# An attention and feed-forward block on one core: load order, maxima turned in blocks on VectorE, and value products in pairs

## The chip, the cores and the metric

The kernel runs on one core of a Trainium2 chip. The metric is the device time of one execution in microseconds; of several runs the median is taken. TensorE (PE) multiplies, VectorE (DVE) and ScalarE (ACT) read its results in PSUM, GpSimd (POOL) works on SBUF alone here, and SyncE (SP) issues most of the DMAs.

## The reference

x has four batches of 512 rows with 512 features. All of it is fp32.

```python
q = rotary((x @ Wq + bq) in 16 heads of 32);  k = rotary(x @ Wk + bk);  v = x @ Wv + bv   # one k and v for all heads
attn = softmax(q k^T / sqrt(32));  ctx = attn @ v
x = layernorm(x + ctx @ Wo + bo)
quantize(w) = clip(round(w / (mean(|w|) + 1e-8)), -1, 1)
h = sigmoid(x @ quantize(w1).T) * (x @ quantize(w2).T)      # 1408 hidden features
x = layernorm(x + h @ quantize(w3).T)
```

## The kernel before

The kernel is written out step by step; every instruction is pinned to the order in which the program issues it, so each engine and each DMA queue works strictly in that order. A helper records the instructions, so most of them have line 75 (VectorE, ScalarE, GpSimd), 80 (matmuls), 83 (DMAs of SyncE) or 86 (transposes) in the profile.

**Steps.** A step (b, c, t) is one of 64: batch b, a group c of four heads, a block t of 128 keys. The main loop (lines 855 to 894) does in each step: the scores of all 512 queries against the 128 keys for four heads (`scores`, line 404), then the value products of the step before (`weigh`, line 445), and in batch 0 the sums of its exponentials by matmuls against ones (`count`, line 454). For later batches GpSimd adds the exponentials up (`total`).

**Scores.** `scores` fills two PSUM tiles `ps` of two heads each: 32-row matmuls against kT, and onto them a two-row matmul with `negm`, which takes the row maximum off. ScalarE then writes the exponentials `es` (1024 columns at a time). `weigh` multiplies `es` with v into four column strips of `acc`; `count` does the same into `den`.

**Maxima.** The maximum of each query's scores is found seven steps ahead (LEAD = 7, `find_maxima`, line 812): matmuls into `pmax`, and a reduction `mx` on VectorE. For batch 0 these are 32-row matmuls (`row_maxima`), later full ones from a split q (`maximum`, line 371). Four chunks of 128 queries per step are taken as two pairs; a pair has a tile of the same two-buffer pool as `ps` (tag "sc"). A single chunk takes the tile of tag "den" (one buffer). Once the next-to-last projection is past (`batches[-1].done < NC` is false, from about step 26) the maxima stand 1-2-1 with fill work between them (lines 886 to 893).

**Spreading the maxima.** `spread` (line 385) turns the 128x16 maxima of a group by a PE transpose into a tile `pm` of the two-buffer pool "mm"; ScalarE negates them, VectorE takes the rest that the rounded type leaves, and two DMAs carry them through DRAM into `negm`, two rows for each head.

**Fill.** Between these, `fill.draw(pace)` takes pieces of other work, each about 1.8 us of PE: projections of later batches (`project_in`: pk, pq, followed by a rotation of four or five VectorE operations, `turn`, line 238), the output projection `po`, and the feed-forward products `gu` and `po`. All their PSUM tiles come from "mm". `quantize(n)` (line 777) draws jobs that load, sum and quantize the feed-forward weights: ACT makes `sgn`, VectorE makes `raw` from it; after step 16 `sgn` is put into the PSUM bank "den" (line 210). `due()` starts late work such as `normalize` (line 461; reductions `part`, small operations `few`), `store_q` and loads, by counted slots, twice a step.

**Start.** 24 fp32 matmuls of ones warm PE up (`WARM`, lines 53 and 152). Meanwhile SyncE issues all loads in the order of lines 129 to 144: biases, k/v weights, four chunks of xT, the first q weights, cos, sin, the rest.

The main loop's part for the maxima and the fill, as before:

```python
        if batches[-1].done < NC:

            find_maxima(n + LEAD, 0, 1)
            begin_middle()
            due()
            find_maxima(n + LEAD, 2, 3)
            quantize(1)
            fill.draw(pace)
            quantize(1 if b == 0 or n % 3 == 0 else 0)
```

Of the kernel before, what the change touches and what calls it, by code (L numbers as in the profile page):

```python
# [10 lines left out]
F32 = mybir.dt.float32  # L11
F32R = mybir.dt.float32r
BF16 = mybir.dt.bfloat16
I32 = mybir.dt.int32
AF = mybir.ActivationFunctionType
ALU = mybir.AluOpType
# [4 lines left out]
P = 128  # L21
HD = 32
# [6 lines left out]
def postln_block(  # L29
# [15 lines left out]
    nc = tc.nc  # L45
    B, T, D = x.shape
    NC = D // P
    NT = T // P
    NF = wf.shape[1]
    NG = P // HD  # L50
    SCALE = 1.0 / float(HD) ** 0.5
    W = 512
    WARM = 24

    const = ctx.enter_context(tc.tile_pool(name="const", bufs=1))
    small = ctx.enter_context(tc.tile_pool(name="small", bufs=2))
# [10 lines left out]
    pin = tc.keep_in_program_order  # L67
# [14 lines left out]
    def move(out, in_):  # L82
        pin(nc.sync.dma_start(out=out, in_=in_))  # L83

    def transpose(out, in_, identity):
        pin(nc.tensor.transpose(out, in_, identity))
# [31 lines left out]

    chunks = iter([(b, c) for b in range(B) for c in range(NC)])

    def load_xT(n):

        for _ in range(n):
            b, c = next(chunks, (None, None))
            if b is not None:
                batches[b].xT.append(work.tile([P, T], F32, tag="xT", name="xT", bufs=6))
                move(batches[b].xT[c], xT[b, :, c, :])

    move(bkv_sb, bkv)
    move(bq_sb, bq)  # L130
    move(wkv_sb, wkv)
    load_xT(NC)
    move(wq_sb[0], wq[:, 0])
    move(cos_sb, cos)
    move(sin_sb, sin)
# [22 lines left out]
    def quantized():  # L158

        order = ((0, False), (1, False), (0, True), (2, False), (1, True), (2, True))
        jobs = [(m, last, f) for m, last in order for f in range(NF)]

        means = {}
        for n, (m, last) in enumerate(order):
            if not last:
                for k, step in ((2, 0), (6, 1), (10, 2)):
                    means[(n + 1) * NF + k] = (m, step)
        raws, part, row, pg, hi, waiting = {}, {}, {}, {}, {}, []  # L170

        def load(k):
            if k < len(jobs):
                m, _, f = jobs[k]

                tag, bufs = ("wd", 5) if k % 2 else ("wg", 4)
                raws[k] = wp.tile([P, W], F32, tag=tag, name="raw", bufs=bufs)
                pool.dma_start(out=raws[k], in_=wf[m, f])

        def mean(m, step):  # L180
            if step == 0:
                row[m] = small.tile([P, 1], F32, tag="row", name="row")
                dve.tensor_reduce(row[m], part[m], AX.X, ALU.add)
            elif step == 1:
                pg[m] = ps_mm.tile([P, 1], F32, tag="mm", name="pg")
                mm(pg[m], ones, row[m], True, True)
                gamma = small.tile([P, 1], F32, tag="gamma", name="gamma")
                act.activation(gamma, pg[m], AF.Identity, scale=1.0 / (NF * W * P), bias=eps_q)
                row[m] = gamma
            else:  # L190
                hi[m] = small.tile([P, 1], F32, tag="hi", name="hi")
                act.mul(hi[m], row[m], 0.5)

        AHEAD = 4
        for k in range(AHEAD):
            load(k)
        for k, (m, last, f) in enumerate(jobs):
            load(k + AHEAD)
            if k in means:
                mean(*means[k])  # L200
            raw = raws.pop(k)
            if not last:
                if f == 0:
                    part[m] = small.tile([P, NF], F32, tag="part", name="part", bufs=3)
                junk = work.tile([P, W], BF16, tag="th", name="junk")
                act.activation(junk, raw, AF.Abs, accum_out=part[m][:, f : f + 1])
            else:
                if now > PER:

                    sgn = ps_acc.tile([P, W], F32, tag="den", name="sgn")  # L210
                else:
                    sgn = work.tile([P, W], BF16, tag="th", name="sgn")
                act.activation(sgn, raw, AF.Sign, bias=hi[m])
                dve.scalar_tensor_tensor(raw, raw, hi[m], sgn, ALU.is_gt, ALU.min)
                waiting.append((kept[m][f], raw))
            if len(waiting) > 2 or k + 1 == len(jobs):
                for w, q in waiting[: 1 if k + 1 < len(jobs) else 3]:
                    pool.dma_start(out=w.bitcast(F32), in_=q)
                del waiting[:1]
            yield  # L220
# [164 lines left out]
    def spread(b, c):  # L385


        s = batches[b]
        pm = ps_mm.tile([NG * NT, P], F32, tag="mm", name="pm")
        transpose(pm, s.mx[c].rearrange("p i t -> p (i t)"), ident)  # L390
        m = small.tile([NG * NT, 2, P], F32R, tag="m", name="m")
        mH, mL = m[:, 0, :], m[:, 1, :]
        act.mul(mH, pm, -1.0)
        dve.scalar_tensor_tensor(mL, pm, -1.0, mH.bitcast(F32), ALU.mult, ALU.subtract)
        s.negm[c] = work.tile([P, T], F32R, tag="negm", name="negm", bufs=3)
        yield
        rows = dram.tile([2, NG, T], F32, tag="rows", name="rows", bufs=3)
        move(rows.rearrange("n i (t k) -> (i t) n k", k=P), m.bitcast(F32))
        yield
        for n in range(2):  # L400
            move(s.negm[c].bitcast(F32).rearrange("(i r) k -> i r k", r=HD)[:, n], rows[n])
        yield

    def scores(b, c, t):
# [40 lines left out]
    def weigh(b, c, t, es):  # L445
        s = batches[b]
        if t == 0:
            s.acc = ps_acc.tile([P, T], F32, tag="acc", name="acc")
            s.ctxT[c] = work.tile([P, T], F32, tag="ctxT", name="ctxT", bufs=6)
        columns(s.acc, s.v[:, t, :], es, t == 0, t == NT - 1)  # L450
        if t == NT - 1:
            act.copy(s.ctxT[c], s.acc)

    def count(b, c, t, es):

        s = batches[b]
        if t == 0:
            s.den = ps_acc.tile([P, T], F32, tag="den", name="den")
        columns(s.den, ones[:, 0:HD], es, t == 0, t == NT - 1)
# [317 lines left out]
    def quantize(n):  # L777
        for _ in range(n):
            next(weights, None)
# [12 lines left out]
    def due():  # L792

        nonlocal slot
        slot += 1
        for entry in list(late):
            if slot >= entry[0] and next(entry[1], "end") == "end":
                late.remove(entry)
# [13 lines left out]
    def find_maxima(k, *chunks):  # L812

        if k >= len(steps):
            return
        b, c, i = steps[k]
        if chunks[0] == 0:
            ask(k + HEADS)
            while batches[b].done <= c or (b and k not in heads):
                if batches[b].done <= c:  # L820
                    fill.one()
                else:
                    begin_middle()
                    due()
                    ask(k)
        if b == 0:
            row_maxima(b, c, i, chunks[0] // 2)
        else:
            maximum(b, c, i, chunks, heads[k])
        if i == NG - 1 and chunks[-1] == NT - 1:  # L830

            late.insert(0, (slot + (1 if now < 0 else 2), spread(b, c)))
# [18 lines left out]
            move(bo_sb, bo.partition_broadcast(P))  # L851
        quantize(3)

    last = None
    for n, (b, c, t) in enumerate(steps):
        now = n
        pace = (1.8, 3.8, 4.8, 4.6)[b]
        if t == 1 and PER <= n + NT - 1 < len(steps):
            load_q(*steps[n + NT - 1][:2])
        es = scores(b, c, t)  # L860
        if last is not None:
            weigh(*last)
        if last is not None and last[0] == 0:
            count(*last)
        last = (b, c, t, es)
        if n == NC * NT // 2:

            late.append((slot, load_x(0)))
        if t == NT - 1:
            begin = slot + 3  # L870
            late.append((begin, normalize(b, c)))
            if c == NC - 1:
                late.append((begin + 7, feed(b)))
                if b > 0:
                    late.append((slot + 6, load_x(b)))
        if batches[-1].done < NC:

            find_maxima(n + LEAD, 0, 1)
            begin_middle()
            due()  # L880
            find_maxima(n + LEAD, 2, 3)
            quantize(1)
            fill.draw(pace)
            quantize(1 if b == 0 or n % 3 == 0 else 0)
        else:
            find_maxima(n + LEAD, 0)
            fill.draw(0.4 * pace)
            find_maxima(n + LEAD, 1, 2)
            begin_middle()
            due()  # L890
            fill.draw(0.3 * pace, True)
            find_maxima(n + LEAD, 3)
            fill.draw(0.3 * pace)
        due()
    weigh(*last)
    now = len(steps)
    while fill.gens or fill.urgent or late:
        fill.draw(3.0)
# [66 lines left out]
```

## Time and profile before

| what | before |
|---|---|
| three runs | 670.8, 672.12, 674.28 us |
| profiled execution, its own time | 672.56 us |
| its span, first to last instruction | 670.8 us |
| granted TensorE clock, mean | 0.997 |
| DMA moved, mean rate | 107.78 MB, 161 GB/s |
| PE matmuls of gate, up (`gu`) | 704 records, 172.9 us busy |
| `pmax` full, 32-row | 192 and 128 records, 75.2 and 25.7 us |
| `acc`, `den` | 512 and 128 records, 68.2 and 16.7 us |
| `pm` transposes | 16 records, 4.4 us |
| DVE reductions `mx` | 159, 158.1 us |

An fp32 matmul has two records, an fp32r one has one. A busy time is the union of the spans of a group, so overlapping matmuls are not counted twice. A line of the timeline has start, duration, engine, line, operation, the tile written and the tiles read, shapes, and how many; in brackets the idle time of the engine before it and what ended that. Times are in us from the start of the span. A step is named by its number n from 0 to 63, its start is that of its first `ps` matmul.

### The profile page before, as it was taken

Reading aid. Unit: us, or ns where it says so; the run is one execution under the profiler, and the core shown is the slowest. Engines: PE = TensorE matmul, PEld = TensorE weight load, DVE = VectorE, ACT = ScalarE, POOL = GpSimd, SP = SyncE. Lnnn points to the kernel's source line nnn. Section 1 sums busy time; section 2 is a strip of 40 time slices with the busy share of each in tenths; the row PEclk is TensorE's granted clock in tenths of the full one; section 3 lists DMA queues with packets and bytes.
Section 4 is the critical chain, followed back from the end, with each engine's and each line's share of the span. In section 5 each row is a group of like instructions: output and inputs, shape, how many; then the busy total and the mean of one; then the engine's idle time right before and its main releaser. Section 6 shows DMA issues by size and latency. Waiting matters only on the chain.

```text
span 670.8 us, 9406 instructions
## 1 busy us (share of the span) xinstructions
PE 644.7 (96%) x3222; PEld 358.5 (53%) x3222; DVE 430.0 (64%) x619; ACT 282.8 (42%) x441; POOL 324.4 (48%) x414
## 2 busy tenths in 40 slices
PE   9989999999999989999999899999999999999995
PEld 6333333443333355665456466654555685778884
DVE  1896766587787867766666966676635553464335
ACT  1466555655443644333334445233435421234213
POOL 0615334535987776376666375576574802202000
PEclk9999999999999999999999999999999999999998
DMA  8755668688575286355132456351232364236531
GB/s 283 248 192 175 205 199 261 186 286 276 162 245 172 92 259 202 116 169 162 54 84 82 125 164 215 124 172 29 73 100 67 126 217 148 79 109 213 183 107 63
DMA packets 60671, 107.78 MB, mean 161 GB/s; under 512 B 14592, under 2 KB 15360, under 8 KB 60624
## 3 DMA queue, kind: packets, MB, share of 16 engines
q1 hardware_dynamic: 52560, 81.10, 38.5%
q0 software_dynamic: 7920, 25.96, 11.8%
q8 instruction: 25, 0.41, 0.3%
q14 instruction: 22, 0.18, 0.1%
q10 hardware_dynamic: 144, 0.13, 0.1%
HBM read 84.06 MB, written 23.10 MB: 160 GB/s over the span
## 4 chain that ended last, share of the span: by engine, by line
PE 81%; DVE 9%; DMA 4%; ACT 3%; issue 2%; SPq 1%; POOL 0%; DVEq 0%; ACTq 0%; POOLq 0%
PE gu L80 23%; PE po L80 19%; PE ps L80 11%; PE pmax L80 8%; PE acc L80 7%; PE pq L80 7%; DVE mx L75 3%; PE den L80 2%; DMA wg<-w 2%; ACT es L75 2%; PE pk L80 1%; DVE xt L75 1%; PE warm L80 1%; SPq L83 1%; DMA xT<-in_xT 1%
## 5 line engine op out<-in xcount | busy, mean ns | idle before, releaser
L75 DVE TENSOR_REDUCE mx<-pmax 128x1 f32<-128x512 f32 (+1 forms) x159 | 158.1, 1007 | 81.3 <-PE pmax L80 81.1
L75 ACT ACTIVATE es<-ps 128x1024 f32<-128x1024 f32 x128 | 124.2, 1022 | 141.9 <-PE ps L80 133.9
L80 PE MATMUL gu<-y,wg 128*128 128x512 f32 x704 | 172.9, 395 | 2.0 <-DMA wg<-w 1.1
L80 PEld LDWEIGHTS gu<-y,wg 128*128 128x128 f32 x704 | 131.1, 188 | 38.4 <-issue 4.7
L75 POOL TENSOR_TENSOR total<-total,es 128x512 f32<-128x512 f32 x96 | 123.8, 1319 | 45.2 <-ACT es L75 45.1
L80 PE MATMUL po<-wd,h 128*128 128x512 f32 x352 | 87.0, 395 | 4.2 <-DVE y L75 2.9
L75 POOL TENSOR_TENSOR total<-es 128x512 f32<-128x512 f32 x48 | 60.5, 1290 | 55.8 <-ACT es L75 55.8
L80 PE MATMUL pmax<-kr,qr 128*128 128x512 f32 x192 | 75.2, 455 | 3.7 <-ACT es L75 2.2
L80 PEld LDWEIGHTS po<-wd,h 128*128 128x128 f32 x352 | 64.9, 188 | 22.5 <-DVE y L75 4.6
L75 ACT CAST h<-hw 128x512 fp32r<-128x512 f32 x44 | 27.3, 620 | 100.7 <-DVE hw L75 100.7
L80 PE MATMUL acc<-es,v 128*32 128x512 f32 x512 | 68.2, 605 | 0.0
L80 PEld LDWEIGHTS pmax<-kr,qr 128*128 128x128 f32 x192 | 33.6, 188 | 57.0 <-ACT es L75 20.9
L75 DVE SCALAR_TENSOR_TENSOR hw<-th,gu 128x512 f32<-128x512 f32 x44 | 30.2, 687 | 46.9 <-PE gu L80 46.8
L80 PE MATMUL po<-wo_sb,ctxT 128*128 128x512 f32 x128 | 58.9, 593 | 0.3 <-DVE hw L75 0.3
L80 PE MATMUL ps<-negm,ones_r 2*128 2x512 f32 x256 | 58.2, 788 | 0.0
L75 DVE SCALAR_TENSOR_TENSOR xt<-po,xt 128x512 f32<-128x512 f32 x48 | 32.8, 684 | 38.1 <-PE po L80 38.1
L75 DVE TENSOR_TENSOR h<-hw,h 128x512 fp32r<-128x512 f32 x44 | 42.1, 957 | 21.7 <-ACT h L75 21.4
L80 PE MATMUL ps<-qT,kT 32*128 32x512 f32 x384 | 55.6, 640 | 0.0
L75 POOL DMA_DIRECT2D raw<-in_wf x66 | 36.1, 549 | 37.4 <-DMA w<-raw 26.7
L80 PE MATMUL pq<-xT,wq_sb 128*128 128x512 f32 x112 | 53.0, 601 | 1.0 <-ACT v L75 1.0
L75 ACT ACTIVATE th<-gu 128x512 f32<-128x512 f32 x44 | 26.3, 598 | 49.1 <-PE gu L80 49.0
L80 PEld LDWEIGHTS po<-wo_sb,ctxT 128*128 128x128 f32 x128 | 24.1, 189 | 22.0 <-issue 19.2
(98 smaller groups left out, 639.2 us busy)
## 6 DMA issues: line engine op xcount, KB each, us to landing
wg<-w SPq DMA_DIRECT2D x88, 256.0 KB
raw<-in_wf POOLq DMA_DIRECT2D x66, 256.0 KB, 4.6
qr<-qp SPq DMA_DIRECT2D x96, 128.0 KB
wd<-w SPq DMA_DIRECT2D x44, 256.0 KB
w<-raw POOLq DMA_DIRECT2D x33, 256.0 KB, 4.9
qp<-q SPq DMA_DIRECT2D x48, 128.0 KB
rden<-flat SPq DMA_DIRECT2D x64, 64.0 KB
xt<-in_x SPq DMA_DIRECT2D x16, 256.0 KB
```

The costliest lines, as they stand in the source:

```text
L75: return lambda *args, **kw: pin(getattr(self.engine, name)(*args, **kw))
L80: pin(nc.tensor.matmul(out, lhsT=lhsT, rhs=rhs, start=start, stop=stop))
L83: pin(nc.sync.dma_start(out=out, in_=in_))
```

## The change

- **Warming** is 10 matmuls instead of 24.
- **Loads**: the four xT chunks of batch 0 go alternately on ACT's and SP's queue; the biases follow them on ACT's queue instead of standing first on SP's.
- **Maxima**: VectorE negates the 128x16 maxima, takes the rest, and turns both in 32x32 blocks (`turned`). PE's transpose, the "mm" tile and ACT's operation go. The DMAs carry pieces of 32 numbers.
- **Order of a step**: in batch 0 the fill stands ahead of the maxima in odd steps and behind them in even ones; from batch 1 on (step 16) every step has the 1-2-1 form, with `quantize` in it.
- **Value products**: every even step issues, behind its scores, the products (and sums) of the two steps before; odd steps issue none.
- **`sgn`** after step 16 is a bf16 tile in SBUF (tag "rot_a") instead of the bank "den".

```diff
-    WARM = 24
+    WARM = 10
...
+    def load_xT(n, engines=(nc.sync,)):
...
+                pin(engines[k % len(engines)].dma_start(out=batches[b].xT[c], in_=xT[b, :, c, :]))
...
-    move(bkv_sb, bkv)
-    move(bq_sb, bq)
     move(wkv_sb, wkv)
-    load_xT(NC)
+    load_xT(NC, (nc.scalar, nc.sync))
+    pin(nc.scalar.dma_start(out=bkv_sb, in_=bkv))
+    pin(nc.scalar.dma_start(out=bq_sb, in_=bq))
...
-                    sgn = ps_acc.tile([P, W], F32, tag="den", name="sgn")
+                    sgn = work.tile([P, W], BF16, tag="rot_a", name="sgn", bufs=1)
...
-        pm = ps_mm.tile([NG * NT, P], F32, tag="mm", name="pm")
-        transpose(pm, s.mx[c].rearrange("p i t -> p (i t)"), ident)
-        m = small.tile([NG * NT, 2, P], F32R, tag="m", name="m")
-        mH, mL = m[:, 0, :], m[:, 1, :]
-        act.mul(mH, pm, -1.0)
-        dve.scalar_tensor_tensor(mL, pm, -1.0, mH.bitcast(F32), ALU.mult, ALU.subtract)
+        mx = s.mx[c].rearrange("p i t -> p (i t)")
+        m = small.tile([P, 2, NG * NT], F32R, tag="m", name="m")
+        turned = small.tile([P, HD], F32, tag="turned", name="turned")
+        dve.tensor_scalar(m[:, 0, :], mx, -1.0, None, ALU.mult)
+        dve.scalar_tensor_tensor(m[:, 1, :], mx, -1.0, m[:, 0, :].bitcast(F32), ALU.mult, ALU.subtract)
+        dve.transpose(turned, m.rearrange("p n k -> p (n k)").bitcast(F32))
...
-        rows = dram.tile([2, NG, T], F32, tag="rows", name="rows", bufs=3)
-        move(rows.rearrange("n i (t k) -> (i t) n k", k=P), m.bitcast(F32))
+        rows = dram.tile([P // HD, 2, NG, NT, HD], F32, tag="rows", name="rows", bufs=3)
+        move(rows.rearrange("o n i t k -> (o n i t) k"), turned)
         yield
+        to = s.negm[c].bitcast(F32).rearrange("(i r) (t o k) -> i r t o k", r=HD, t=NT, o=P // HD)
         for n in range(2):
-            move(s.negm[c].bitcast(F32).rearrange("(i r) k -> i r k", r=HD)[:, n], rows[n])
+            move(to[:, n], rows[:, n].rearrange("o i t k -> i t o k"))
...
+    def weigh_held():
+        for one in held:
+            weigh(*one)
+        for one in held:
+            if one[0] == 0:
+                count(*one)
+        held.clear()
...
         es = scores(b, c, t)
-        if last is not None:
-            weigh(*last)
-        if last is not None and last[0] == 0:
-            count(*last)
-        last = (b, c, t, es)
+        if t % 2 == 0:
+            weigh_held()
+        held.append((b, c, t, es))
...
-        if batches[-1].done < NC:
-
+        if b == 0:
+
+            if t % 2:
+                fill.draw(pace)
             find_maxima(n + LEAD, 0, 1)
             begin_middle()
             due()
             find_maxima(n + LEAD, 2, 3)
             quantize(1)
-            fill.draw(pace)
-            quantize(1 if b == 0 or n % 3 == 0 else 0)
+            if t % 2 == 0:
+                fill.draw(pace)
+            quantize(1)
         else:
             find_maxima(n + LEAD, 0)
+            quantize(1)
             fill.draw(0.4 * pace)
             find_maxima(n + LEAD, 1, 2)
             begin_middle()
             due()
+            quantize(1 if n % 3 == 0 else 0)
             fill.draw(0.3 * pace, True)
             find_maxima(n + LEAD, 3)
             fill.draw(0.3 * pace)
         due()
-    weigh(*last)
+    weigh_held()
```

More of the change, by code (lines that the diff above doesn't have):

```diff
@@ L119, in postln_block @@
     chunks = iter([(b, c) for b in range(B) for c in range(NC)])
-    def load_xT(n):
-        for _ in range(n):
+    def load_xT(n, engines=(nc.sync,)):
+        for k in range(n):
             b, c = next(chunks, (None, None))
@@ L126, in load_xT @@
                 batches[b].xT.append(work.tile([P, T], F32, tag="xT", name="xT", bufs=6))
-                move(batches[b].xT[c], xT[b, :, c, :])
-    move(bkv_sb, bkv)
-    move(bq_sb, bq)
+                pin(engines[k % len(engines)].dma_start(out=batches[b].xT[c], in_=xT[b, :, c, :]))
     move(wkv_sb, wkv)
-    load_xT(NC)
+    load_xT(NC, (nc.scalar, nc.sync))
+    pin(nc.scalar.dma_start(out=bkv_sb, in_=bkv))
+    pin(nc.scalar.dma_start(out=bq_sb, in_=bq))
     move(wq_sb[0], wq[:, 0])
@@ L852, in postln_block @@
         quantize(3)
-    last = None
+    held = []
+    def weigh_held():
[5 more added lines that the diff above has]
+        held.clear()
     for n, (b, c, t) in enumerate(steps):
```

## The prediction

> **What bounds the kernel now.** I read the page first, then busy time by stage, then TensorE (PE) and VectorE (DVE) instruction by instruction in two steps of each stage.
>
> ```profile
> PE 644.7 (96%) x3222; PEld 358.5 (53%) x3222; DVE 430.0 (64%) x619; ACT 282.8 (42%) x441; POOL 324.4 (48%) x414
> ```
>
> PE is busy for 96% of the span. "Busy" counts from start to modelled end, so a PE that waits inside a row of matmuls still looks busy, and shares alone do not show what an edit is worth. The next view has the stages that I use: the start (until the first scores), A (steps 0 to 15, batch 0), B (16 to 27), C (28 to 57, the rest of the maxima), and the end.
>
> ```profile
> core 0: us, PE busy (x) PEld busy (x) DVE busy (x) ACT busy (x) POOL busy (x), PEclk, DMA share, GB/s
> 0.00:48.20 48.20, 44.48 (x163) 21.42 (x163) 30.67 (x42) 19.61 (x52) 14.64 (x33) 1.00 0.74 252
> 48.20:154.80 106.60, 105.64 (x613) 40.14 (x612) 75.03 (x105) 62.52 (x106) 47.23 (x67) 1.00 0.67 213
> 154.80:244.50 89.70, 84.25 (x404) 33.95 (x403) 71.86 (x102) 43.42 (x62) 71.30 (x87) 1.00 0.63 200
> 244.50:489.20 244.70, 238.75 (x1253) 137.65 (x1253) 164.41 (x225) 97.77 (x131) 145.61 (x154) 1.00 0.42 128
> ```
>
> In A and B, DVE is 70% and 80% busy. There it can be what PE waits for. One step of A, on PE, and the maxima that DVE takes beside it:
>
> ```profile
> 130.66 1.06 PE L80 MATMUL acc<-es,v 128*32 128x512 f32 x8
> 131.54 1.04 PE L80 MATMUL den<-es,ones 128*32 128x512 f32 x8
> 132.51 1.20 PE L80 MATMUL pmax<-kr,qr 128*128 128x512 f32 x4
> 133.55 1.88 PE L80 MATMUL pq<-xT,wq_sb 128*128 128x512 f32 x4
> 135.35 1.13 PE L80 MATMUL ps<-room,kT 32*128 32x512 f32 x6
> ...
> 136.99 1.06 PE L80 MATMUL acc<-es,v 128*32 128x512 f32 x8
> ```
>
> ```profile
> 133.28 2.35 DVE L75 TENSOR_REDUCE mx<-pmax 128x2 f32<-128x1024 f32 x2 [3.31 <-PE pmax L80]
> ```
>
> The reader is to see a ring. `pmax` and `ps` share two PSUM buffers. From `pmax` (132.51) DVE needs until 135.63 for both maxima; only then may the second `ps` tile be written, and `acc` starts 1.34 later, at 136.99. So from `pmax` to the next step's `acc` it takes 4.48 us, whatever PE does in between: `pq` (1.81) and the scores (1.30) fit in. For the maxima of batch 0 (32-row matmuls) the same distance is 4.88 (78.81 to 83.69). The step is this distance plus `acc` and `den`, 1.85.
>
> **Stage A.** The order of instructions of the changed kernel shows its pairs. Even step: scores, 8 `acc`, 8 `den` matmuls, `pmax`, half a projection. Odd step: scores, half a projection, `pmax`, and then at once the next even step's scores. From the rows: two `acc` and two `den` together are 3.57 (4 x 0.86 streamed, 0.13 less than 2 x 1.85); `pmax` to the end of the odd scores 4.48; half a projection 1.81; `pmax` to the even `acc` again 4.48. Sum 14.34, against 2 x (1.85+4.48) = 12.66. The projection of the odd step used to lie beneath the ring and now lies ahead of it: +1.68 a pair. Over the seven pairs of steps 2 to 15: three with 4.88 twice, one mixed, three with 4.48 twice, 45.4+14.8+43.0 = 103.2. To this I add 1.2 for the negation and turning of the maxima, which in steps 5, 9 and 13 stands between the two reductions (0.4 each, see below), and 1.2 for four pairs in which a weight's `raw` (0.74) is queued ahead of them (0.3 each). 105.6; the trace has 93.0 from 63.5 to 156.5. Step 1 gains 0.3. **A: +12.3.** In this 93.0 the losses by the transpose `pm` (it splits four concurrent matmuls into two groups: step 5 took 7.96, its neighbours 6.6 and 6.4) are already inside.
>
> **Stage B.** Now the maxima stand 1-2-1 between fill work, with the single ones in the `den` bank. That takes the waits for exponentials away: step 21 took 7.57, a step of C with the same content in 1-2-1 form (38) took 6.85. Without new waits B would take 12 scores of 1.30, 6 `acc` pairs of 1.88, one `den` pair of 1.74, maxima of 1.12 a step and the trace's 43.4 of fill (0.9 of it the wait of step 16's single `pmax` until ACT has copied `den`): 85.4 for 89.3, so -3.9. But the order on DVE puts a whole rotation between the maxima of the first chunk and those of the pair:
>
> ```profile
> 136.22 0.74 DVE L75 SCALAR_TENSOR_TENSOR a<-pq,bq_sb,cos_sb 128x512 f32<-128x512 f32 x1
> ...
> 137.62 0.76 DVE L75 SCALAR_TENSOR_TENSOR pq<-pq,bq_sb,sin_sb 128x512 f32<-128x512 f32 x1
> 138.47 0.69 DVE L75 TENSOR_TENSOR q<-a,pq 128x512 f32<-128x512 f32 x1
> ```
>
> From 136.22 to 139.16 a rotation is 2.94; it starts when PE is at the pair's `pmax`, and the pair's reduction (1.22) comes behind it, 4.3 us after that `pmax`. PE is back at the second `ps` after 2.57. That is 1.7 lost in step 16, 2.5 in 17 (the rotation of k has five instructions, 3.6), 1.2 in 18 and 3.5 in 19, where the second half of the pair's cover has no fill. Steps 20, 22 and 24 have `part` (1.24), statistics (0.87) or the rotation ahead of the last single maximum: 1.3, 0.4 and 2.1 at the following `pmax`; 2 more in 25 and 26; 0.9 is a longer wait for `xT` in 17. These are 15.6; where one wait takes up another, 13.1 are left, so the whole of it gives +9.2. Bounds -3.9 and +9.2; the stalls are read from the order, so I take near the upper end, **B: +8**.
>
> **Stage C.** Three parts. First, `pm` goes:
>
> ```profile
> 256.58 0.27 PE L86 MATMUL pm<-ident,mx 128*16 128x128 f32 x1
> 257.13 1.65 PE L80 MATMUL gu<-y,wg 128*128 128x512 f32 x6 [0.28 <-DVE hw L75]
> ```
>
> It takes one of two `mm` banks, so the next `gu` waits for DVE. The steps with it are longer than those without by 0.71, 0.62, 0.11, 0.62, 0.63, 0.63, 0.66 and 0.9: -4.9. Second, pairing: one `acc` group alone is 1.00, and 0.88 when another follows. 37 groups remain before, 38 in 19 pairs after: 37.0 against 35.7, -1.3. Third, what the removed `acc` covered in odd steps. The single `pmax` behind it needs the `den` bank, so the last reduction of the step before:
>
> ```profile
> 252.76 0.68 DVE L75 TENSOR_REDUCE mx<-pmax 128x1 f32<-128x512 f32 x1
> ```
>
> ```profile
> 417.29 0.50 PE L80 MATMUL pmax<-kr,qr 128*128 128x512 f32 x1 [0.64 <-DVE mx L75]
> ```
>
> In step 49 this wait exists already, behind `acc`. Without `acc`, PE arrives 1.30 after its scores began. In steps 29, 31, 39, 41, 43 and 45 the reduction ends 1.83, 1.75, 2.16, 1.76, 1.72 and 1.48 after it (29: scores 251.6, reduction until 253.44): waits of 0.63, 0.55, 0.96, 0.56, 0.52, 0.28, and 1.05 more than now in 49 and 53. +5.6; it is 0 if DVE's order is kinder, 11.2 if every wait doubles. **C: -0.6.**
>
> **Start.**
>
> ```profile
> 1.50 8.43 PE L80 MATMUL warm<-ones 128*128 128x128 f32 x48 [1.50 <-POOL ones L75]
> 9.77 3.60 PE L80 MATMUL pk<-xT,wkv_sb 128*128 128x512 f32 x8
> ```
>
> `pk` stands behind the warming matmuls, and the chain to the first maxima behind `pk`. Of 48 warming records 20 stay; at the first ones' spacing (14 in 3.0 us) PE is free at 5.9. The last `xT` chunk landed at 9.01 in the trace; with two queues and without two small loads ahead it lands about 0.9 earlier, so `pk` could end at 9.0 instead of 13.2. Nothing gained and 4.4 gained (with 0.7 for a `pm` at 37.0) are the bounds. The first matmuls ran at half pace: 14 records in the first 3.0 us, 22 in the last 2.2, and the pace changed 5.9 us after the first one, when the changed kernel's warming is just over. So `pk` starts at that half pace; I take **-3.5**.
>
> [...]
>
> **The small parts.** `sgn` in SBUF instead of PSUM: DVE's `raw` takes 0.74 in steps 12 to 16 with an SBUF `sgn` and 0.74 in steps 18 to 24 with the PSUM one: nothing. The turned maxima: ACT loses 0.27, DVE has three operations instead of one of 0.27; the nearest rows are `few` on 128x16 (0.24) and this `m`, so I take 0.2 each, 0.3 to 0.4 more in one step of four, counted in A. Their DMA now moves 128-byte pieces (128, then 2 x 64) instead of 512 and 2048; it is issued at 258.42 and 262.72 for scores at 273.6, so 10 us hide it. If that cover went, its chunk's scores would wait. Nothing is queued behind it on SP that is due sooner than before. Four loads move from SP's queue to ACT's ahead of its first work, at about 0.45 each by SP's rows; ACT's first use of them is at 13.4, which hides that. End: same work, 0.
>
> **Sum**, on the profiled execution's 672.56 (span 670.8): -3.5 +12.3 +8 -0.6 = 688.8; the median is 0.4 lower, so **688.4**.
>
> **Rivals.** (1) Faster: the ring's 4.48 is no floor, since PE's own work between (1.03+1.81+1.30) is 4.14, and DVE is soon enough when the projection is moved. Then A is -3.5 (0.9 by pairs, 2.6 by `pm`), B -3.9, C -6.2, start -3.5: 655. It decides if `pmax` to `acc` in odd steps is under 2.8. Against it: 2.35 of DVE and 1.34 behind it are measured. 0.1. (2) Only A loses, and neither B nor C waits: 672.6-3.5+12.3-3.9-6.2 = 671. 0.1. (3) A and C as forecast, B without waits: 677. 0.2. (4) All at the bad ends, start -0.5, B +9.2, C +5: 698.7. 0.1. Forecast, 683 to 694: 0.5. The range 674 to 697 holds the forecast, (3) and half of (4). This kernel can be told from no change by about 0.5% (3.4 us): faster 0.1, same 0.1, slower 0.8.
>
> **What would show it.** Right: in A odd steps that end with `pmax` directly ahead of `ps`, and 2 us of missing PE work there, pairs of 14 to 15.5; in B DVE's rotation between two `mx`; in C `pmax` waiting for `mx` in odd steps; no `gu` waiting behind `pm`. Wrong: pairs of A under 13, or a start that is not 2 us shorter.

## The result, and the profile after

The changed kernel takes 715.76 us (median of 6 runs, 709.35 to 717.52) against 671.66 us (6 runs on the same chip): ratio 1.0633, 95% interval 1.0598 to 1.0667. The profiled execution took 717.52 us, its span is 715.7, and TensorE's mean granted clock is 0.961 instead of 0.997. The direction was forecast, the size was not: 688.4 was said, and the range ended at 697.

From the page of the changed kernel:

```profile
PE 665.4 (93%) x3178; PEld 368.3 (51%) x3178; DVE 450.3 (63%) x661; ACT 280.5 (39%) x425; POOL 329.0 (46%) x414
```

PE is 20.7 us longer busy for the same products. No new work explains that. The view by stage (us; busy time of PE, PEld, DVE, ACT, POOL with counts; then the granted clock) says where to look:

```profile
0.00:44.80 44.80, 42.20 (x134) 18.07 (x134) 30.70 (x44) 19.43 (x51) 14.64 (x33) 1.00 0.79 271
44.80:177.30 132.50, 119.47 (x593) 43.06 (x592) 76.60 (x113) 62.32 (x102) 46.77 (x65) 0.90 0.56 176
177.30:287.20 109.90, 93.96 (x408) 38.79 (x408) 84.89 (x118) 43.66 (x60) 75.22 (x89) 0.94 0.51 158
287.20:532.10 244.90, 236.17 (x1245) 141.50 (x1244) 170.12 (x241) 95.82 (x123) 145.00 (x153) 0.99 0.42 128
532.10:715.70 183.60, 173.64 (x801) 126.92 (x800) 87.95 (x148) 59.31 (x92) 47.36 (x77) 0.98 0.40 129
```

The length of each stage, against the forecast:

| stage | before | after | difference | forecast |
|---|---|---|---|---|
| start | 48.2 | 44.8 | -3.4 | -3.5 |
| A (steps 0 to 15) | 106.6 | 132.5 | +25.9 | +12.3 |
| B (16 to 27) | 89.7 | 109.9 | +20.2 | +8 |
| C (28 to 57) | 244.7 | 244.9 | +0.2 | -0.6 |
| end | 181.6 | 183.6 | +2.0 | 0 |
| span | 670.8 | 715.7 | +44.9 | +16.2 |

A and B have the whole miss, and they have the lowest clock. PE's waits, summed (us, times, longest):

```profile
PE ps L80 <- DVE mx L75: 18.4, 15, 3.4
PE pmax L80 <- DVE mx L75: 11.8, 13, 1.7
```

Before, `ps` had no such row, and `pmax` waited 1.1 us in all for `mx`. So the new waits are those that were forecast, on VectorE's maxima. But they do not account for 44.9 by themselves. One pair of A (steps 5 and 6), on PE:

```profile
91.40 1.13 PE L80 MATMUL ps<-room,kT 32*128 32x512 f32 x4 [1.31 <-DVE mx L75]
93.04 1.22 PE L80 MATMUL ps<-room,kT 32*128 32x512 f32 x2 [0.52 <-DVE mx L75]
...
95.48 3.64 PE L80 MATMUL acc<-es,v 128*32 128x512 f32 x16
98.89 2.33 PE L80 MATMUL den<-es,ones 128*32 128x512 f32 x16
```

and the pair before it (steps 3 and 4):

```profile
78.58 1.92 PE L80 MATMUL acc<-es,v 128*32 128x512 f32 x16
80.32 1.90 PE L80 MATMUL den<-es,ones 128*32 128x512 f32 x16
```

The same 16 matmuls take 3.64 us instead of 1.92. Cut into windows of 3.41 us, the stretch shows why. The columns are: stretch, its length, busy time of PE, PEld, DVE, ACT and POOL with counts, and then the granted clock, the DMA share and GB/s.

```profile
89.40:92.81 3.41, 1.81 (x12) 0.30 (x4) 3.08 (x6) 1.78 (x4) 2.88 (x5) 1.00 0.17 19
92.81:96.23 3.42, 3.19 (x12) 1.04 (x16) 1.50 (x3) 1.02 (x1) 1.03 (x2) 0.52 0.92 305
96.23:99.64 3.41, 3.41 (x20) 0.79 (x16) 0.00 (x0) 0.00 (x0) 0.54 (x1) 0.50 0.90 320
```

In the first window PE waits, and is busy for 1.81 of 3.41 us. In the next two its clock is half. The six runs agree: the quickest, 709.35 us, had a mean clock of 0.974, the slowest, 717.52, 0.961. Such stretches of one or two windows stand in A at 58.8, 92.9, 113.4, 130.5 and 161.2, all on one grid of 3.41 us, 27.3 us together; in B there are 13.7 us. Before, there were none in A, B and C.

### The profile page after: what moved, and what is told of

It reads as the page before. It is cut to its first block, busy times and chain, and to the rows that moved or that the text cites. A ratio compares the mean times of both kernels' runs of the same rounds, so it can differ in the third digit from the quotient of the medians.

```text
span 715.7 us, 9339 instructions
## 1 busy us (share of the span) xinstructions
PE 665.4 (93%) x3178; PEld 368.3 (51%) x3178; DVE 450.3 (63%) x661; ACT 280.5 (39%) x425; POOL 329.0 (46%) x414
## 4 chain that ended last, share of the span: by engine, by line
PE 70%; DVE 19%; DMA 3%; issue 2%; SPq 2%; ACT 2%; POOL 1%; DVEq 0%; ACTq 0%; POOLq 0%
PE gu L80 21%; PE po L80 16%; PE ps L80 9%; PE acc L80 8%; DVE mx L75 7%; PE pmax L80 7%; PE pq L80 4%; SPq L83 2%; PE den L80 2%; PE pk L80 2%; DVE part L75 2%; DVE raw L75 1%; DVE pq L75 1%; DVE xt L75 1%; DVE a L75 1%
## 5 line engine op out<-in xcount | busy, mean ns | idle before, releaser
L80 PEld LDWEIGHTS gu<-y,wg 128*128 128x128 f32 x704 | 132.5, 189 | 35.1 <-issue 2.4
L80 PE MATMUL pmax<-kr,qr 128*128 128x512 f32 x192 | 85.0, 498 | 13.0 <-DVE mx L75 11.6
L80 PE MATMUL po<-wd,h 128*128 128x512 f32 x352 | 89.2, 403 | 3.8 <-DVE y L75 3.4
L80 PEld LDWEIGHTS po<-wd,h 128*128 128x128 f32 x352 | 66.8, 193 | 21.9 <-DVE y L75 6.1
L80 PE MATMUL acc<-es,v 128*32 128x512 f32 x512 | 71.8, 685 | 0.0
L80 PE MATMUL ps<-qT,kT 32*128 32x512 f32 x384 | 63.3, 642 | 7.6 <-DVE mx L75 7.4
L75 ACT CAST h<-hw 128x512 fp32r<-128x512 f32 x44 | 27.3, 620 | 106.4 <-DVE hw L75 106.4
L80 PEld LDWEIGHTS pmax<-kr,qr 128*128 128x128 f32 x192 | 36.3, 192 | 63.1 <-issue 28.7
L80 PE MATMUL ps<-negm,ones_r 2*128 2x512 f32 x256 | 65.1, 783 | 0.0
L80 PE MATMUL po<-wo_sb,ctxT 128*128 128x512 f32 x128 | 60.8, 603 | 0.0
L75 DVE TENSOR_TENSOR h<-hw,h 128x512 fp32r<-128x512 f32 x44 | 37.7, 857 | 21.0 <-ACT h L75 20.7
L75 POOL TENSOR_TENSOR q<-q,q 128x512 fp32r<-128x512 f32 x12 | 15.2, 1264 | 61.3 <-ACT q L75 60.9
```

The source lines that it names most:

```text
L75: return lambda *args, **kw: pin(getattr(self.engine, name)(*args, **kw))
L80: pin(nc.tensor.matmul(out, lhsT=lhsT, rhs=rhs, start=start, stop=stop))
```

## The experiments

The theory from the profile: the waits have the forecast length, and the rest is PE's half clock behind them. Rivals: the pairs wait longer than forecast; the turned maxima or `sgn` in SBUF slow VectorE. Stage lengths are from each run's profile (start, A, B, C, end).

| kernel | median, us | ratio to before (95%) | stages | half clock in A, B, C |
|---|---|---|---|---|
| after | 715.76 | 1.0633 (1.0598 to 1.0667) | 44.8, 132.5, 109.9, 244.9, 183.6 | 27.3, 13.7, 6.8 |
| x1_unpaired | 685.9 | 1.0202 (1.0163 to 1.0242) | 43.7, 108.3, 109.1, 239.8, 181.1 | 0, 20.5, 0 |
| x2_pairs_from_16 | 690.85 | 1.0265 (1.0231 to 1.0298) | 44.3, 108.0, 109.5, 244.7, 182.5 | 0, 13.7, 6.8 |
| x3_filler | 703.17 | 1.0455 (1.0425 to 1.0484) | 44.7, 119.7, 108.7, 241.8, 184.8 | 0, 10.2, 0 |
| x4_sgn_sbuf | 673.24 | 1.0026 (0.9996 to 1.0056) | 47.0, 106.6, 90.7, 243.5, 181.6 | 0, 3.4, 0 |
| x5_b_as_before | 668.85 | 0.9940 (0.9907 to 0.9974) | 44.1, 110.0, 94.6, 240.0, 181.6 | 3.4, 3.4, 0 |
| x6_spread_later | 717.48 | 1.0649 (1.0589 to 1.0710) | 44.5, 126.2, 122.6, 241.9, 182.5 | 20.5, 34.0, 3.5 |
| x7_pair_forward | 680.81 | 1.0106 (1.0063 to 1.0149) | 44.1, 110.3, 101.7, 239.3, 181.2 | 3.4, 13.7, 0 |
| x8_turned_alone | 671.41 | 0.9987 (0.9957 to 1.0018) | 46.6, 111.9, 90.2, 240.0, 181.6 | 6.8, 0, 0 |
| x9_mixed | 665.01 | 0.9887 (0.9863 to 0.9912) | 44.1, 106.5, 90.3, 240.9, 181.6 | 0, 0, 0 |
| x10_warm_10 | 670.27 | 0.9978 (0.9953 to 1.0003) | 45.5, 106.6, 90.0, 244.5, 181.6 | 0, 0, 0 |
| x11_loads_only | 672.48 | 1.0005 (0.9980 to 1.0029) | 46.9, 106.6, 90.4, 244.3, 181.6 | 0, 0, 0 |
| x12_no_sums_b1 | 680.94 | 1.0106 (1.0073 to 1.0139) | 43.7, 109.9, 105.4, 238.5, 181.2 | 3.4, 13.7, 0 |
| x13_filler_b | 688.49 | 1.0234 (1.0198 to 1.0271) | 44.3, 110.3, 111.2, 239.0, 181.2 | 3.4, 13.7, 0 |
| x14_filler_no_sums | 678.63 | 1.0107 (1.0048 to 1.0167) | 43.7, 108.3, 102.2, 239.4, 181.2 | 0, 0, 0 |

**x1_unpaired**, the changed kernel without pairs:

```diff
-        if t % 2 == 0:
-            weigh_held()
+        weigh_held()
...
-            if t % 2:
-                fill.draw(pace)
...
-            if t % 2 == 0:
-                fill.draw(pace)
+            fill.draw(pace)
```

> The changed kernel without its pairs: every step issues the value products of the step before, and in batch 0 the fill stands behind the maxima in every step, as before the change; loads, warming, turned maxima, sgn in SBUF and the 1-2-1 form from step 16 stay. Theory G (the pairs open waits of PE on the maxima, and these waits close the clock gate): no half clock between the start and the last step, 100.4 or less for stage A, 652 to 668 us. Rival S (it is another part, the sgn tile in SBUF or the small pieces of DMA, that makes DVE late): 685 or more, with half-clock windows in stage B.

685.9 is outside what the first of these gave, and A is 108.3, not 100.4 or less. It is inside the rival's number, which named `sgn` or the DMA pieces as the cause; x4_sgn_sbuf and x5_b_as_before ask that. A is nearly as before (+1.7), so the pairs made A's loss. But B keeps its whole loss without them (+19.4), so B's cause is another. C is 239.8, 4.9 shorter than before.

**x2_pairs_from_16**: pairs only from step 16 on (`if b == 0 or t % 2 == 0: weigh_held()`, the fill of batch 0 behind the maxima).

> The changed kernel with pairs only from step 16 on; batch 0 as before the change. Theory G: stage A costs 98 to 101 us instead of 127, stage B and C stay as in the changed kernel, so 715.8 - 28 = 688, 683 to 693. Rival (stage B's waits follow from the late start out of stage A): B recovers too, 670 or less.

The time is as expected, though A is 108.0 and not 98 to 101. A is free of the loss, and C loses 4.9 against x1_unpaired: that is the price of pairs in C with the clock that they close there (6.8 us at half clock).

**x3_filler**: all of the change, and two zero-weight matmuls in each odd step of batch 0, where PE would wait for the maxima.

```diff
+            if t % 2:
+                for _ in range(2):
+                    mm(open_bank[0], zeros, open_bank[1], False, False)
```

> The changed kernel with MORE work: in each of the eight odd steps of batch 0, two fp32 matmuls of zero weights are added onto the open projection tile, behind the maxima, where PE waits for DVE; they add zero. 16 matmuls, 13.7 us of PE at full clock. Theory G: they lie inside the waits, keep the clock open, and the four pairs with a half clock (19.6, 19.0, 17.6 and 18.6 instead of about 15.5, 15.5, 15.1 and 14.7) recover: 715.8 - 14 = 702, 698 to 706, with no half clock in stage A. Rival W (the waits alone are the loss, the clock only shows them): 716 to 722.

PE has more to do, and the kernel is 12.6 us faster. The groups of `ps` and `acc` in stage A, after:

```profile
L80 PE MATMUL ps<-room,kT 32*128 32x512 f32 x128 | 31.2, 676 | 11.0 <-DVE mx L75 11.0
...
L80 PE MATMUL acc<-es,v 128*32 128x512 f32 x112 | 21.3, 902 | 0.0
```

and in x3_filler:

```profile
L80 PE MATMUL ps<-room,kT 32*128 32x512 f32 x128 | 27.0, 639 | 0.7 <-DVE mx L75 0.6
...
L80 PE MATMUL acc<-es,v 128*32 128x512 f32 x112 | 13.5, 598 | 0.0
```

The idle 11.0 us are filled, the clock is 1.00 through all of A, and one `acc` takes 598 ns instead of 902. VectorE's work and order are the same. A is 119.7: 13.1 over before, where 12.3 was forecast. So the other 12.8 of A's 25.9 is the clock.

C has no filler in this run, and yet it is 241.8 instead of 244.9. All steps of C but two are as long as in the changed kernel to 0.02 us. The two are 35 and 49, first in the changed kernel, then in x3_filler (the columns are those of the windows above):

```profile
341.32:350.95 9.63, 7.97 (x34) 5.33 (x33) 3.67 (x5) 3.23 (x5) 4.30 (x4) 0.82 0.86 242
457.62:468.80 11.18, 9.54 (x41) 6.82 (x40) 7.32 (x12) 2.48 (x3) 4.99 (x4) 0.85 0.34 111
```

```profile
327.27:335.42 8.15, 6.63 (x34) 4.12 (x33) 3.92 (x5) 3.22 (x5) 3.03 (x3) 1.00 0.87 259
442.10:451.68 9.58, 7.94 (x41) 5.69 (x40) 7.44 (x12) 2.47 (x3) 5.03 (x4) 1.00 0.37 115
```

So of the price of pairs in C (5.1 against x1_unpaired) 3.1 is one window of half clock in each of these two steps, and 2.0 is left with the clock open.

**x6_spread_later**: `spread` is queued with `slot + 3` instead of `slot + 2`. In the changed kernel the slow pairs were 1+2, 5+6, 9+10 and 13+14 (7+8 had one window at half clock too and took 16.7), just those with the three turning operations between the two reductions; this takes them out from there.

> The changed kernel, but the three VectorE operations that negate and turn the maxima come a half step later, so not between the two reductions of the odd steps 5, 9 and 13. Theory G (some 0.5 us of added wait in those steps tips PE's clock): no half clock in A, pairs of A all 14 to 15.5, A about 118 to 120 instead of 132.5, time 701 to 705. Rival H (the pairs' waits alone close the clock, wherever these three operations stand): A stays at 130 or more, 713 to 718.

The rival is the nearer one: the time is in its range, but A, 126.2, is below its 130, with 20.5 us at half clock instead of 27.3. The three operations moved, and the same four pairs are slow (18.5, 18.6, 16.2 and 16.4). The windows of the pair 5+6 in this run:

```profile
88.67:92.09 3.42, 2.10 (x16) 0.60 (x10) 3.15 (x4) 1.67 (x4) 3.00 (x5) 1.00 0.58 144
92.09:95.50 3.41, 3.41 (x18) 0.75 (x15) 1.34 (x5) 1.02 (x1) 0.91 (x2) 0.50 0.90 297
```

Here PE was even busier in the window that tips the clock (2.10 of 3.42). The half clock begins at 58.0, 92.1 and 126.2, ten windows (34.1 us) apart, and a slow pair and the quick one behind it together take 33.6 to 33.7 us here, 34.2 in the changed kernel: so long the grid and the pairs stay nearly in step. The fourth begins at 156.9, nine windows on. PE waits 1.32 us in step 6 and again in step 8; the first wait has half clock behind it, the second has not. So which pair is hit seems to depend on how its waits lie on the grid, and not on 0.5 us of VectorE's work alone; the place on the grid was not varied by itself. That a second effect of this edit made B longer (122.6) was not looked into.

**x4_sgn_sbuf**: the kernel before with nothing but `sgn` in SBUF after step 16.

> The kernel before with one edit: sgn in SBUF (bf16) instead of the PSUM bank den from step 17 on. In the changed kernel the operation raw took 1.3 to 3.4 us there at times instead of 0.74. If raw waits for GpSimd's use of SBUF, raw lengthens here too, but no maximum is queued behind it on the path: 672 to 676. Rival (the length of raw comes from the changed order alone): raw stays at 0.74 and the time at 671 to 673. If this edit is the main loss: 685 or more.

In the time it is nothing that can be told. In the rows it is not nothing. `raw` before, and in this run (all 33; mean in ns):

```profile
L75 DVE SCALAR_TENSOR_TENSOR raw<-raw,hi,sgn 128x512 f32<-128x512 f32 x33 | 24.1, 738 | 0.4 <-ACT sgn L75 0.4
```

```profile
L75 DVE SCALAR_TENSOR_TENSOR raw<-raw,hi,sgn 128x512 f32<-128x512 f32 x33 | 32.3, 987 | 0.3 <-ACT sgn L75 0.3
```

The order of before hides 8 us more of VectorE. What a `raw` does where it is not hidden, on DVE and on POOL in x1_unpaired:

```profile
218.62 3.38 DVE L75 SCALAR_TENSOR_TENSOR raw<-raw,hi,sgn 128x512 f32<-128x512 f32 x1
```

```profile
216.49 4.95 POOL L75 TENSOR_TENSOR total<-total,es 128x512 f32<-128x512 f32 x4
```

`raw` begins during GpSimd's four sums and ends 0.56 us after them, 3.38 us for what takes 0.74 elsewhere; the reduction behind it starts only at 221.92. The means go the same way: 738 ns with `sgn` in PSUM, 987 and 1011 (after) with it in SBUF, and one `raw` of 5.49 us in x13_filler_b. There, too, GpSimd made four sums (189.44 to 194.38), and `raw` ended 1.04 us after them. The four sums here are four instructions of 1.3 us, and `raw` ends behind the last of them, not behind one; a shorter operation, `m` in step 9 of x5_b_as_before (1.19 us), ends at 112.47, with the one GpSimd addition that it began beside (112.44). It is not so in every case: at 191.12 in x1_unpaired a `raw` took 1.58 us and ended 2.34 us ahead of the last of four sums. What decides this was not found out. Where a `raw` is held up in this way, it is called the lock below.

**x7_pair_forward**: without pairs, and in B the pair of maxima is issued right behind the single one, ahead of the fill.

```diff
+            early = batches[-1].done < NC
+            if early:
+                find_maxima(n + LEAD, 1, 2)
             fill.draw(0.4 * pace)
-            find_maxima(n + LEAD, 1, 2)
+            if not early:
+                find_maxima(n + LEAD, 1, 2)
```

> The changed kernel without pairs; in steps 16 to about 26 the pair of maxima is issued right behind the single one, with no fill between them, so that no rotation stands between these two reductions on DVE. Theory O (the rotation between the reductions is what the scores wait for): B falls from 109 to 92 to 100, time 669 to 677. Rival Q (any 1-2-1 form loses there, because the den bank and the number of DVE operations hold it): B stays at 104 or more, 681 to 688.

Between the two. B falls by 7.4, to 101.7, where theory O wanted 9 to 17, and the time, 680.81, is just under the rival's 681 to 688. The rotation now stands ahead of the last single maximum, and PE meets it there (step 18):

```profile
177.42 1.65 PE L80 MATMUL pmax<-kr,qr 128*128 128x512 f32 x3 [3.40 <-DVE mx L75]
178.86 3.62 PE L80 MATMUL pq<-xT,wq_sb 128*128 128x512 f32 x4
```

The 3.40 us are waited for the reduction behind five instructions for k. `pq` behind it takes 3.62 instead of 1.88: half clock.

**x5_b_as_before**: without pairs, and the maxima of B in two pairs, the loop's condition as before (`if batches[-1].done < NC`).

> The changed kernel without pairs, and with the maxima of steps 16 to about 26 in two pairs again, as before; new loads, turned maxima, sgn in SBUF and the rest stay. Theory O (the order of the maxima in B, with DVE's rotation between them, made the 20 us of B; pairs made A): start -3.5 to -4.5, A +1 to +2, B -1 to +1, C -5, so 663 to 667. Rival P (the loss of B comes from the turned maxima or from sgn in SBUF, which slow DVE there): B stays above 100 us and the time is above 676.

668.85 is just above 663 to 667, and 0.6% faster than before. B is 94.6, 14.5 less than in x1_unpaired: the 1-2-1 order is the main cause there. It is not quite 89.7, and A is 110.0; in both, PE ran one window at half clock behind a turning operation that GpSimd held up (`m` took 1.19 us in steps 9 and 17, 0.17 when undisturbed). The profiled run took 672.14 us; the ten runs go from 664.09 at a mean clock of 0.996 to 673.75 at 0.986, so in the median run less of this is to be expected.

**x8_turned_alone**: the kernel before with nothing but the turned maxima.

> The kernel before with nothing but the turned maxima (three VectorE operations and the finer DMA pieces in place of PE's transpose, the bank and ACT's operation). From the changed kernel without pairs: A +1 to +2, B about 0, C -4 to -5, so 668 to 670 (ratio 0.994 to 0.998). Rival: the C gain came from the 1-2-1 form with sgn in SBUF, not from the missing transpose; then 672 to 675.

C is 4.7 shorter, as expected, and not by the 1-2-1 form, as the rival said. But the median, 671.41, lies between the two expectations and is no better than before. In the profiled run A is 5.3 longer, with two windows of half clock behind one late maximum (at 117.5). That the median is kept up by the same thing is likely, not shown.

**x10_warm_10** and **x11_loads_only**: the kernel before, with only the shorter warming, or only the new loads.

> The kernel before with 10 warming matmuls instead of 24 and nothing else. Theory W (the warming held up the first product, the loads came in time): start 2 to 3.5 us shorter. Rival L (the last load of the first chunks sets it): start shorter by 0 to 1, since the loads land as late as before.

> The kernel before with the new order and queues of the first loads and still 24 warming matmuls. Theory W: start within 0.5 us of before. Rival L: start 2 to 3.5 us shorter.

With 10 warming matmuls and the old loads:

```profile
1.49 4.64 PE L80 MATMUL warm<-ones 128*128 128x128 f32 x20 [1.49 <-POOL ones L75]
6.52 4.13 PE L80 MATMUL pk<-xT,wkv_sb 128*128 128x512 f32 x8 [0.39 <-DMA xT<-in_xT]
```

With 24 and the new loads:

```profile
1.49 7.12 PE L80 MATMUL warm<-ones 128*128 128x128 f32 x48 [1.49 <-POOL ones L75]
8.45 3.60 PE L80 MATMUL pk<-xT,wkv_sb 128*128 128x512 f32 x8
```

The shorter warming is worth 2.7 us of start in the profile (the ratio of the whole times, 0.9953 to 1.0003, can't tell it from nothing); the loads are then late by 0.39. In the second run `pk` stands right behind the warming, as before, so earlier loads can't move it; its start is 1.3 shorter because the 48 records took 7.12 us and not 8.43, so by estimate from these two numbers the full pace came earlier in this execution. Theory W allowed 0.5 there. By the medians (1.0005) the loads alone do nothing. Both together: 3.4 in the changed kernel, where the 20 warming records took 4.63 us, nearly as in x10_warm_10 (4.64), so behind a short warming the loads gave 0.7. The 4.1 of x9_mixed has a part of the kind just told: there they took 4.07.

**x12_no_sums_b1**, **x13_filler_b** and **x14_filler_no_sums** take B apart, all from x1_unpaired. The first leaves out GpSimd's sums of batch 1 after the second key block; the second puts zero-weight matmuls where PE waits; the third does both.

```diff
+            if j == 1:
+                for _ in range({17: 1, 18: 2, 19: 1, 20: 3, 23: 1}.get(now, 0)):
+                    mm(pss[0][:, 0, :], zeros, cos_sb, False, False)
...
-            else:
+            elif b > 1:
                 for j in range(2):
                     for i in range(2):
                         pool.tensor_tensor(
```

> The changed kernel without pairs; GpSimd leaves out the sums of exponentials of batch 1 after the second key block (so batch 1's softmax lacks them). Theory K (in steps 16 to 26 DVE's operations with two SBUF inputs wait until GpSimd's are done, and that is a large part of B's 20 us): the weights' operation is back near 0.74 us each in batch 1, B falls from 109 to 97 to 102, time 673 to 679. Rival O (the order alone: a rotation between the maxima): B stays at 105 or more, 682 to 687.

> The changed kernel without pairs, with eight zero-weight matmuls (0.86 us each) in all, in steps 17 to 20 and 23, each where PE would wait for the second score tile. Theory C (the waits of B close the clock, and the half clock behind them is a large part of B's 20 us): the half clock of steps 18 to 20 goes, B falls from 109 to 100 to 104, time 675 to 680. Rival D (DVE's order alone is what B waits for; PE at half clock only fills the waits): B stays at 106 to 111, 683 to 689.

> Both at once: the changed kernel without pairs, the eight zero-weight matmuls in steps 17 to 20 and 23, and batch 1 without the sums of exponentials after the second key block (its softmax lacks them). Without the sums alone B was 105.4. Theory C (with the 5.49 us lock of the weights' operation away, an open clock is worth what the half clock of 13.7 us took, up to 6.9): no half clock in steps 17 to 22 and B 98 to 102, time 672 to 678. Rival D (VectorE's order alone sets the steps): B 104 to 108, 679 to 685.

Without the sums `raw` in B is 960 ns instead of 1250, and B is 105.4, 3.7 shorter: theory K, which wanted 97 to 102 and `raw` near 0.74, falls. Not all of the 3.7 is the lock. Step 17 became 1.65 shorter; here it is in x1_unpaired, then in x12_no_sums_b1:

```profile
163.60 0.70 PE L80 MATMUL ps<-qT,kT 32*128 32x512 f32 x2 [0.70 <-DVE mx L75]
...
164.90 1.72 PE L80 MATMUL acc<-es,v 128*32 128x512 f32 x8
```

```profile
165.16 0.70 PE L80 MATMUL ps<-qT,kT 32*128 32x512 f32 x2 [0.71 <-DVE mx L75]
...
166.44 1.07 PE L80 MATMUL acc<-es,v 128*32 128x512 f32 x8
```

PE's wait is the same, but in x1_unpaired a window of half clock follows it. So it is in step 26, 0.70 shorter with a wait of 1.54 and 1.55. The lock has what is left, 1.3, most of it in step 23 (1.14), behind the `raw` of 3.38. x13_filler_b could not tell: steps 17 to 19 became 3.7 shorter, and then in step 20 a `raw` of 5.49 us brought a wait of 4.36 and a new half clock; by itself its number speaks for theory D. With both, PE's clock is open in all of B:

```profile
152.00:254.20 102.20, 94.14 (x419) 38.80 (x418) 78.06 (x118) 43.17 (x59) 45.53 (x64) 1.00 0.56 175
```

Steps 18 and 20 went from 13.96 and 13.86 (x12_no_sums_b1) to 10.70 and 10.68, 6.4 together. In steps 17, 19 and 23 there was less wait than filler, so that those became 3.2 longer; 102.2 holds this. The median, 678.63, lies between the two expectations, the stage just above theory C's 98 to 102.

**x9_mixed**: the parts that gained. New loads and 10 warming matmuls; until the last projection (about step 26) the PE transpose, `sgn` in PSUM and two pairs of maxima as before; from then on the turned maxima; no paired value products.

```diff
     def spread(b, c):
...
+        if batches[-1].done < NC:
+            pm = ps_mm.tile([NG * NT, P], F32, tag="mm", name="pm")
+            transpose(pm, s.mx[c].rearrange("p i t -> p (i t)"), ident)
...
+            return
         mx = s.mx[c].rearrange("p i t -> p (i t)")
```

> The kernel before, with only those parts of the change that gained: new loads and 10 warming matmuls, and the turned maxima from the last projection on (about step 26); before that the transpose by PE, and sgn in the PSUM bank as before; no pairs, and the maxima in two pairs until then. By the lengths of the runs so far: start -3.5 to -4, A 0, B 0, C -4.7, so 663 to 665 (ratio 0.987 to 0.990). Rival: the parts take from each other (the clock's windows fall otherwise, or a load comes late), then 666 to 670.

665.01 us, at the upper end of the 663 to 665 expected, 1.1% faster than before and 7% faster than the changed kernel. By stage:

```profile
0.00:44.10 44.10, 40.38 (x137) 17.09 (x137) 30.71 (x44) 19.76 (x52) 14.59 (x33) 1.00 0.79 275
44.10:150.60 106.50, 105.54 (x613) 40.09 (x612) 75.25 (x105) 62.43 (x106) 47.49 (x66) 1.00 0.67 213
150.60:240.90 90.30, 84.41 (x406) 33.95 (x405) 71.87 (x102) 43.46 (x62) 71.49 (x88) 1.00 0.62 200
240.90:481.80 240.90, 235.53 (x1247) 137.65 (x1246) 173.58 (x241) 95.59 (x123) 143.97 (x154) 1.00 0.43 130
```

A and B are those of before, the start is 4.1 shorter and C 3.8, and the clock never closes ahead of the end.

## Why the prediction was wrong, point by point

**Start, -3.5.** Right: -3.4, and the mechanism too (the warming was ahead of `pk`). `pk` took 4.43 us (3.60 before), at first at half pace, as forecast: its records start 0.85 us apart up to 7.62 and 0.43 from there on.

**Stage A, +12.3.** The ring was read rightly. The pairs that ran at full clock took 15.22 (3+4) and 14.32 (11+12); the forecast's terms give 15.14 and 14.34. With the clock kept open A is +13.1. What failed is that the waits of 1 to 2 us in each pair were priced as waits alone. They also close PE's clock, and the next one or two windows run at half pace: pairs 1+2 and 5+6 took 19.0, 9+10 17.6, 13+14 18.6. That is 12.8 us, the largest part of the miss. The prediction spoke of a half pace at the start and did not carry it to the waits that it had itself just forecast.

**Stage B, +8, bounds -3.9 to +9.2.** The order (a rotation of VectorE between the maxima) does cost what was read, at the upper bound: taking from x1_unpaired's +19.4 the lock of 1.3 and the clock of 8.8 (6.4, and 2.4 in steps 17 and 26) leaves 9.3. That it comes so near to 9.2 is in part luck, since the single waits agree less: ahead of the scores of steps 17, 18 and 20 they are 0.70, 2.15 and 3.21 us (0.71, 2.15 and 3.43 in the changed kernel), where 1.7, 2.5 and 3.5 were forecast, and the 1.2 forecast for step 19's is not there. Step 18 of x1_unpaired, DVE:

```profile
172.68 1.38 DVE L75 TENSOR_TENSOR kT<-a,pk 96x512 f32<-96x512 f32 x2
174.09 1.22 DVE L75 TENSOR_REDUCE mx<-pmax 128x2 f32<-128x1024 f32 x1
```

and PE:

```profile
175.37 1.22 PE L80 MATMUL ps<-qT,kT 32*128 32x512 f32 x2 [2.15 <-DVE mx L75]
...
177.79 1.94 PE L80 MATMUL acc<-es,v 128*32 128x512 f32 x8
```

The pair's reduction stands behind k's rotation, PE waits 2.15 us for it (2.5 was forecast for k's rotation), and `acc` then takes 1.94, where it takes 1.07 in x14_filler_no_sums. The bounds failed because they held neither the clock nor the lock. The division into 9.3, 1.3 and 8.8 is that of x1_unpaired, whose B is 109.1; that of the changed kernel, 109.9, was not taken apart. It is by the order in which these were taken away; each alone would come out a little otherwise, as x13_filler_b shows.

**Stage C, -0.6.** +0.2, and near to it by luck: one term was too large, and the half clock made up for it. The transpose `pm` gave 4.9 in x1_unpaired and 4.7 in x8_turned_alone, for 4.9 forecast; the waits of `gu` on VectorE (0.9 us in all before) are gone:

```profile
L80 PE MATMUL gu<-y,wg 128*128 128x512 f32 x704 | 172.9, 396 | 1.7 <-DMA wg<-w 1.7
```

Pairing costs 5.1 there, but 2.0 with the clock open (x3_filler), where 4.3 was forecast (5.6 less 1.3); the other 3.1 is half clock in steps 35 and 49. The waits are of the kind that was named. Step 29:

```profile
297.03 0.50 PE L80 MATMUL pmax<-kr,qr 128*128 128x512 f32 x1 [0.52 <-DVE mx L75]
```

It was 0.63 in the forecast, which adds 0.10 to each difference of its list (1.83 less 1.30 is 0.53) without a reason. PE's waits for `mx` in C are 4.9 in all, 1.0 in x1_unpaired. The half clock of step 35 stands behind another wait, of 1.66, for the load of a weight (`wg`); that of step 49 behind one of 1.64 for `mx`.

**End, 0.** +2.0, with 8.4 us at half clock instead of 4.6; no other cause was looked for.

**Small parts at nothing.** One of them was read from the wrong rows: `raw` with `sgn` in SBUF takes 0.74 in steps 12 to 16, where GpSimd has no sums to do; after them it is held up (1317 ns on the mean in B). So are the two operations on `m`, priced at 0.2 each: their means are 424 and 679 ns in the changed kernel, 0.17 and 0.18 us in step 5, where GpSimd computes nothing beside them. Alone they cost nothing that a median shows (x4_sgn_sbuf, x8_turned_alone), in a stage that waits for VectorE they do.

**The rivals.** The three faster ones fell with A and B: none had the clock in A, and none had a wait in B; the fourth, all at the bad ends (698.7), was nearest and still 17 us short, since its bad ends held no half clock either (its terms add up to 698.6).

## What to carry to other kernels

Where a change adds waits of a microsecond or two on TensorE, price the products that come behind them at half clock for the next one or two windows of 3.4 us too: in stage A that doubled the cost (25.9 us for 13.1 with the clock open), and useless matmuls in the waits won 12.6 us back. Before an operand goes from PSUM to SBUF, or a small operation from PE to VectorE, look at what GpSimd does beside it in the same stage, and take the row from there (`raw` had 738 ns before, 1250 in B of x1_unpaired). Take a bundle apart: its gains (4 us of start, 4 to 5 of C) stood beside losses of 46 us, and alone they made a faster kernel.

## What the runs showed of the hardware

Waits far shorter than a window of 3.41 us can close TensorE's clock. In the changed kernel's stage A two waits of 1.31 and 0.52 us, nearly all of them in one window, were enough: PE was busy for 1.81 of its 3.41 us, and the granted clock was 0.52 and 0.50 in the next two. With such waits filled (x3_filler) it was 1.00 through all of A. Over all sixteen profiles (40 to 600 us of each), 47 windows at full clock were followed by one at half clock. PE's recorded busy share in them was between 0 and 85%; no window under 50% left the clock open, none over 86% closed it, and between these both happened. In the changed kernel alone there are 13, at 21 to 85%, while others, from 53% up, left the clock open. So the busy share of the profile alone does not decide it. In A and B, where the products before and between the waits use 32 rows or 32 columns, windows closed at higher shares (61 and 73% in A of x6_spread_later, 85% in A of the changed kernel) than in C of the changed kernel (51 and 52%); whether such products count for less was not tried, and stays open.
